# Joining segment sums to place sums by accumulating transfers on GpSimd's queue

## The chip, the cores and the metric

The kernel runs on one core of a Trainium2 chip. The metric is the device time of one execution in microseconds. The core has five engines with queues of their own: PE (TensorE, matmuls into PSUM), DVE (VectorE), ACT (ScalarE), POOL (GpSimd) and SP (SyncE, which here only issues transfers). Each engine works through its queue in order and waits at an instruction until the semaphores it needs have come.

## The reference

128 graphs of 128 nodes with 64 features pass four graph layers. Each layer normalises its input (layer norm, then relu), computes something over the adjacency, and adds it to `x`. The change concerns layer 0:

```
mask = (adj > 0)
h_in = relu(layernorm(x))
h[b,j,k,:] = relu(h_in[b,j] @ W1a + (h_in[b,j] - h_in[b,k]) @ W1b + b1)      # 192 wide
x[b,j] += (sum over k of mask[b,j,k] * h[b,j,k,:]) @ W2 + deg[b,j] * b2
```

With `p = h_in @ (W1a + W1b) + b1` and `q = -h_in @ W1b` the inner term is `relu(p[j] + q[k])`. For every node j one has to sum it over the neighbours k of j, of which there are about 16 of 128 in this data, though some nodes have many more.

Layers 1 to 3 are graph convolutions: layer 1 is three products with the adjacency with relu between, layer 2 one product, a normalisation of rows and one over the whole batch, layer 3 a product with a tanh network.

## The kernel before, in words

The 128 graphs are worked on in 32 groups of four (`G = 4`, `NG = 32`). The main loop, in `network`, runs over the groups; one stream of **tasks** computes the sums of layer 0, and two **side streams** are woven between.

*Tasks.* Instead of all 128 x 128 pairs, the kernel lists the neighbours of each node. A task takes one neighbour of every node: a one-hot matrix (`oh`, `ohn`) picks the q row, PE adds it onto a PSUM tile `blk` that ACT had filled with `psort` (the p rows, sorted so that nodes with more neighbours come first), and the result goes through relu into a running sum `acc`. There are 20 tasks per group, in the order of the list `ORDER`:

- twelve *near* tasks (4 matmuls each), which take a node's first neighbours from each third of the nodes;
- five *full* tasks (12 matmuls each, since q is kept as three bf16 parts), which take one more neighbour of every place;
- three *segment* tasks (12 matmuls each). The 128 rows are split into segments of 76, 33, 11, 4, 2 and 2 (`SEGS`), and each segment holds the first places again, for their further neighbours. So nodes with many neighbours are given more rows. Their p rows `psort_r` are copies of the first rows of `psort`, made by transfers.

The near and full tasks add into `acc0`, in places; the segment tasks add into `acc1`, in segment rows. In `differences` the first task of `acc0` (L582) and all later ones (L586) run on DVE; the first segment task (`FIRST_R`, n = 13) is a relu on ACT (L584). The segment tasks are n = 13, 16 and 18 of 0 to 19.

PSUM has eight banks: three `blk` tiles of two banks each, in turn for the tasks, and a pool `ps` of two banks, from which every side step takes its matmul's output (`ps_rank`, `ps_q`, `ps_sA` and so on). `fill` (L563) refills a `blk` on ACT two tasks ahead; `make_onehot` (L544, L549) builds the one-hot matrices on DVE three ahead.

*The first side stream*, `prepare(g + 1)`: transposes the next group's adjacency, ranks neighbours (`mT`, `ps_rank`, `leftT`, `degs`), sorts nodes by degree (`ps_key`, `ps_place`) and builds `fro`, the matrix that takes places back to nodes, and `to`, its transpose, as `to_b` in bf16 on POOL. It computes q (`ps_q`, written to DRAM and read back as `near_q`), the numbers `num`, and p (`ps_p`). On POOL it computes `db` and adds it to `x`. `fro_r` has rows of `fro` copied once per segment by six transfers on SP's queue (L455).

*The second*, `after_layer0(g - 1)`: `layer0_end` takes the sums from rows to nodes by matmuls with `fro` (for `acc0`) and `fro_r` (for `acc1`), both onto `ps_sA` and `ps_sB`, multiplies by W2 (`ps_o`) and adds to `x`. Then come `layer1` (`ps_ah`, `ps_ag`, `ps_pr`; its last sum onto `x` is on POOL, L644) and `layer2_norm`.

A loop that counts the estimated PE time (`PACE`) and how late each stream is (`N_PREPARE`, `N_AFTER`, `LASTS`, `LAG`) decides after each half task which side step is written next. The order that each engine then gets is set by the scheduler of the language layer when the kernel is built: it may move an instruction ahead of another of its engine, and it sets the waits. Tiles come from pools with a fixed number of buffers: `edge` has two of each (`acc0`, `fro`), `once` has one (`acc1`, `sA`, `sB`).

After the last group comes an end phase: layer 2's normalisation over the batch and layer 3.

Of the kernel before, what the change touches and what calls it, by code (L numbers as in the profile page):

```python
# [9 lines left out]
F32 = mybir.dt.float32  # L10
# [3 lines left out]
AF = mybir.ActivationFunctionType  # L14
ALU = mybir.AluOpType
# [3 lines left out]
P = 128  # L19
F = 64  # L20
G = 4
NP = G // 2
H0 = 192
# [8 lines left out]

THIRD = 42
NEAR = 4
FULL = 5
BLOCKS = 3
SEGS = [76, 33, 11, 4, 2, 2]
STARTS = [sum(SEGS[:s]) for s in range(len(SEGS))]  # L40
LIKE = 4

NEARS = [(t, i) for i in range(NEAR) for t in range(3)]
OTHERS = [(None, i) for i in range(FULL + BLOCKS)]
ORDER = [(NEARS, OTHERS)[k] for k in (0, 1, 0, 1, 0)] * 4
ORDER = [kind[sum(k is kind for k in ORDER[:n])] for n, kind in enumerate(ORDER)]
FIRST, FIRST_R = 0, ORDER.index((None, FULL))
N_PREPARE, N_AFTER = 15, 26
PACE, LAG = 0.88, 2.5
LATE = 18  # L50
LASTS = 1.9
PARTS = [2, 4, 6, 6, 6, 8]
# [2 lines left out]
W = NP * H0  # L55
# [18 lines left out]
def network(ctx, tc, io, out, over=None, x1=None):  # L74
# [4 lines left out]
    nc = tc.nc  # L79
# [21 lines left out]
    def matmul(o, w, x, **kw):  # L101
        spend(w, math.prod(x.shape[1:]), x.dtype)
        return nc.tensor.matmul(o, w, x, **kw)  # L103
# [165 lines left out]
    edge = ctx.enter_context(tc.tile_pool(name="edge", bufs=2, reuse_waits="tile"))  # L269
    once = ctx.enter_context(tc.tile_pool(name="once", bufs=1, reuse_waits="tile"))  # L270
# [83 lines left out]
    xs = [keep.tile([P, G, F], F32, tag=f"x{g}", name=f"x{g}") for g in range(NG)]  # L354
# [41 lines left out]
    sorts, psorts, accs, loaded = {}, {}, {}, {}  # L396
# [5 lines left out]
    def prepare(g):  # L402

        xt, parts_q = xs[g], proj[g % 2]
# [45 lines left out]
        next(ln)  # L450
        fro = edge.tile([P, G, P], F32, tag="fro", name="fro")
        nc.vector.tensor_scalar(flat(fro), pl, place_p, None, ALU.is_equal)  # L452
        fro_r = edge.tile([P, G, P], F32, tag="fro_r", name="fro_r")
        for n, start in zip(SEGS, STARTS):
            nc.sync.dma_start(fro_r[start : start + n], fro[0:n])  # L455
        next(ln)
        yield
        pr = bank("ps_to")
        for b in range(G):
            transpose(pr[:, b * P : (b + 1) * P], fro[:, b, :], ident)  # L460
        to = once.tile([P, G, P], F32, tag="to", name="to")
# [28 lines left out]
        num = edge.tile([P, G, P], BF16, tag="num", name="num")  # L490
# [24 lines left out]
        psort = edge.tile([P, NP, W], F32, tag="psort", name="psort")  # L515
# [6 lines left out]
        psort_r = once.tile([P, NP, W], F32, tag="psort_r", name="psort_r")  # L522
# [3 lines left out]
        extra = once.tile([P, NP, W], F32, tag="rest", name="extra")  # L526
        for b in range(G):
            nc.scalar.activation(of(extra, b), of(psort, b), AF.Relu, scale=empty[:, g, b : b + 1])
        sorts[g], psorts[g] = (num, num_r, fro, fro_r), (psort, psort_r, extra)


    tasks = [(g, n) for g in range(NG if x1 is None else 0) for n in range(len(ORDER))]
# [32 lines left out]
    def differences(t):  # L565
        g, n = tasks[t]
        o, oh, third = columns(t), onehots.pop(t), ORDER[n][0]
        for b in range(G):
            for part in range(3) if third is None else (third,):
                q = (proj if third is None else near_q)[g % 2][:, part]  # L570
                matmul(of(o, b), oh[:, b, :], of(q, b), start=False, stop=True, skip_group_check=True)
            if b == 0:
                fill(t + 2)
                make_onehot(t + AHEAD)
            if b == 1:
                yield
        kind = in_segments(n)
        if n in (FIRST, FIRST_R):
            accs[g, kind] = (once if kind else edge).tile([P, NP, W], F32, tag=f"acc{int(kind)}", name=f"acc{int(kind)}")
        acc = accs[g, kind]  # L580
        if n == FIRST:
            nc.vector.scalar_tensor_tensor(acc, o, 0.0, psorts[g][2], ALU.max, ALU.subtract)  # L582
        elif n == FIRST_R:
            nc.scalar.activation(acc, o, AF.Relu)  # L584
        else:
            nc.vector.scalar_tensor_tensor(acc, o, 0.0, acc, ALU.max, ALU.add)  # L586
        yield

    def layer0_end(g):
        xt, (_, _, fro, fro_r) = xs[g], sorts[g]  # L590

        pA, pB = bank("ps_sA"), bank("ps_sB")
        sA = once.tile([P, G, P], F32, tag="sA", name="sA")
        sB = once.tile([P, NP, P], F32, tag="sB", name="sB")
        sums = ((accs[g, False], fro, True), (accs[g, True], fro_r, False))
        for b in range(G):
            for acc, f, start in sums:
                matmul(pA[:, b * P : (b + 1) * P], of(acc, b, slice(0, P)), f[:, b, :], start=start, stop=not start)
            if b % 2:
                yield  # L600
        nc.scalar.copy(flat(sA), pA)
        for b in range(G):
            for acc, f, start in sums:
                matmul(pB[b % 2 * F : (b % 2 + 1) * F, b // 2 * P : (b // 2 + 1) * P], of(acc, b, slice(P, H0)), f[:, b, :], start=start, stop=not start)
# [114 lines left out]
    else:  # L719
# [12 lines left out]
        for g in range(NG):  # L732
# [4 lines left out]
            for t in range(g * per, (g + 1) * per):  # L737
                for _ in differences(t):
# [3 lines left out]
                    while side:  # L742
                        late, s = max(((s[2] * s[3] / (nyields * s[4]) - s[1], s) for s in side), key=lambda k: k[0])
# [308 lines left out]
```

## Time and profile before

| | |
|---|---|
| time, median of three runs | 1431.54 us (1428.42 to 1433.82) |
| profiled execution: time | 1435.94 us |
| profiled execution: span | 1434.1 us |
| mean granted TensorE clock | 0.973 |
| setup and first `prepare`, to the first `acc` | 57.5 us |
| main loop, to the last `acc` | 1270 us |
| end phase | the rest |
| transfers | 111 MB, 77 GB/s, 27% of the 16 DMA engines |

The span is the profile's own, from the first instruction to the last; the execution's time has 1.8 us more around it. A busy share is that of the whole span. In the lines of the profile, `out<-in` are the program's names without buffer numbers; L103 is the helper by which all matmuls are written, so tile names tell them apart. An f32 matmul shows as two instructions, and since matmuls are pipelined, the durations of neighbours overlap: their starts tell the pace. "Idle before" is the time in which the engine waited just before instructions of a group, with what ended the wait. SPq is SP's queue of transfers.

### The profile page before, as it was taken

The page shows a single profiled execution, that of the slowest core. Times are in us where ns is not written, and L with a number is a line of the kernel's source. Part 1 is how long each engine was busy: PE and PEld are TensorE (multiplying, and loading weights), DVE is VectorE, ACT ScalarE, POOL GpSimd, SP SyncE. Part 2 cuts the span into 40 slices and gives each one's busy share as a digit, 9 for nine tenths or more (in the row PEclk, how much of TensorE's full clock was granted, in tenths as well). Part 3 has the DMA queues.
Part 4 walks back from the last instruction along what each step waited for, and adds up shares of the span by engine and source line. Part 5 has one row for each costly group of instructions (what it writes and reads, how often), then busy time and mean ns, then how long its engine had stood idle before and what let it go on. Part 6 is the DMA issues. An engine that isn't in the chain of part 4 may idle for free. (4 is left out here: it accounts for less than half of the span.)

```text
span 1434.1 us, 29471 instructions
## 1 busy us (share of the span) xinstructions
PE 1251.2 (87%) x11124; PEld 983.2 (69%) x11124; DVE 1186.8 (83%) x2692; ACT 997.8 (70%) x1883; POOL 179.5 (13%) x258
## 2 busy tenths in 40 slices
PE   3788999899999899899989989989989999895788
PEld 1466777777777777777777777767777777773566
DVE  7688888888888988888888888888888888875973
ACT  1577777777777777667777777777777777753783
POOL 3000000000000000000000000000000000003930
PEclk9899999999999999999999999999999999997889
DMA  4353222222222222212222222222222222200345
GB/s 106 107 124 93 77 81 81 75 80 82 74 81 81 74 74 71 72 51 80 81 76 79 81 81 74 81 72 72 65 81 56 71 71 74 67 16 8 87 111 131
DMA packets 108788, 110.97 MB, mean 77 GB/s; under 512 B 42895, under 2 KB 88220, under 8 KB 108636
## 3 DMA queue, kind: packets, MB, share of 16 engines
q1 hardware_dynamic: 108636, 109.00, 27.4%
q8 instruction: 89, 1.46, 0.5%
q14 instruction: 63, 0.52, 0.1%
HBM read 52.70 MB, written 35.29 MB: 61 GB/s over the span
## 5 line engine op out<-in xcount | busy, mean ns | idle before, releaser
L586 DVE SCALAR_TENSOR_TENSOR acc<-blk,acc 128x768 f32<-128x768 f32 x576 | 544.6, 951 | 86.4 <-PE blk L103 52.5
L563 ACT COPY blk<-psort 128x768 f32<-128x768 f32 x544 | 436.0, 805 | 144.9 <-DVE acc L586 125.7
L103 PE MATMUL blk<-q,oh 128*128 128x192 bf16 x3072 | 333.6, 247 | 35.2 <-ACT blk L563 34.3
L103 PEld LDWEIGHTS <-oh 128*128 128x128 bf16 x3072 | 263.8, 99 | 102.9 <-issue 89.0
L103 PE MATMUL blk<-near_q,ohn 128*128 128x192 bf16 x1536 | 196.2, 247 | 8.9 <-ACT blk L563 8.0
L103 PEld LDWEIGHTS <-ohn 128*128 128x128 bf16 x1536 | 132.4, 98 | 40.4 <-issue 30.6
L670 POOL TENSOR_TENSOR y<-y,nrm 128x256 f32<-128x256 f32 x32 | 24.4, 762 | 600.2 <-DVE acc L586 329.3
L563 ACT COPY blk<-psort_r 128x768 f32<-128x768 f32 x96 | 77.6, 809 | 3.7 <-DVE acc L586 3.7
L103 PEld LDWEIGHTS <-ones_b 3*128 3x128 bf16 (+2 forms) x312 | 30.8, 99 | 63.8 <-issue 57.0
L544 DVE TENSOR_SCALAR ohn<-near_n 128x1536 bf16<-128x1536 bf16 x128 | 73.2, 583 | 0.0
L103 PE MATMUL ps_pr<-g,dT 128*128 128x128 f32 x512 | 72.2, 284 | 0.7 <-ACT dT L629 0.3
L103 PE MATMUL ps_ag<-adjT,msg 128*128 128x128 f32 x512 | 71.6, 283 | 0.0
L103 PEld LDWEIGHTS ps_pr<-g,dT 128*128 128x128 f32 x512 | 62.2, 191 | 8.6 <-issue 5.2
L637 ACT COPY msg<-ps_pr 128x512 f32<-128x512 f32 x64 | 37.3, 584 | 42.5 <-PE ps_pr L103 28.3
L484 POOL TENSOR_TENSOR db<-degs,b_all 128x256 f32<-128x256 bf16 x32 | 19.7, 615 | 366.9 <-DVE degs L429 366.9
L103 PEld LDWEIGHTS ps_ag<-adjT,msg 128*128 128x128 f32 x512 | 62.1, 191 | 4.8 <-ACT msg L637 4.4
L103 PE MATMUL ps_p<-wp,hs 128*128 128x384 f32 x128 | 62.1, 568 | 0.0
L582 DVE SCALAR_TENSOR_TENSOR acc<-blk,extra 128x768 f32<-128x768 f32 x32 | 30.6, 958 | 35.4 <-PE blk L103 34.8
L629 ACT ACTIVATE dT<-ps_ag 128x512 f32<-128x512 f32 x96 | 56.6, 590 | 4.5 <-PE ps_ag L103 4.5
L103 PE MATMUL ps_hm<-ident,h 128*64 128x128 f32 x248 | 43.6, 308 | 14.0 <-ACT h L843 14.0
L108 PE MATMUL ps_to<-ident,fro 128*128 128x128 f32 x128 | 21.9, 296 | 37.3 <-DVE fro L452 37.3
L605 ACT COPY sB<-ps_sB 128x256 f32<-128x256 f32 x32 | 11.9, 372 | 60.8 <-PE ps_sB L103 60.8
(221 smaller groups left out, 2696.4 us busy)
## 6 DMA issues: line engine op xcount, KB each, us to landing
q_dram<-q SPq DMA_DIRECT2D x32, 567.0 KB
near_q<-q_dram SPq DMA_DIRECT2D x96, 189.0 KB
near_n<-n_dram SPq DMA_DIRECT2D x96, 126.0 KB
a<-in_adj_dram SPq DMA_DIRECT2D x32, 256.0 KB
adjT_dram<-adjT SPq DMA_DIRECT2D x32, 256.0 KB
adjT<-adjT_dram SPq DMA_DIRECT2D x32, 256.0 KB
psort_r<-psort SPq DMA_DIRECT2D x32, 228.0 KB
fro_r<-fro SPq DMA_DIRECT2D x32, 152.0 KB
```

The source lines that it names most:

```text
L103: return nc.tensor.matmul(o, w, x, **kw)
L108: return nc.tensor.transpose(o, x, i)
L484: nc.gpsimd.tensor_tensor(db, over_f(degs[:, :, 0]), over_g(b2_all), ALU.mult)
L544: nc.vector.tensor_scalar(oh.rearrange("p t b n -> p (t b n)"), near_n[g % 2].rearrange("p t b n -> p (t b n)"), float(i + 1), None, ALU.i ...
L563: nc.scalar.copy(columns(t), psorts[g][in_segments(n)])
L582: nc.vector.scalar_tensor_tensor(acc, o, 0.0, psorts[g][2], ALU.max, ALU.subtract)
L586: nc.vector.scalar_tensor_tensor(acc, o, 0.0, acc, ALU.max, ALU.add)
L605: nc.scalar.copy(flat(sB), pB[:, 0 : NP * P])
L629: nc.scalar.activation(flat(dT), pa, AF.Relu)
L637: nc.scalar.copy(flat(msg), pm)
L670: nc.gpsimd.tensor_tensor(y, y, over_f(nrm), ALU.mult)
```

## The change

It changes how the segment sums `acc1` reach the nodes, and where two of the three segment tasks are summed.

- `fro_r` and its six transfers go, and with them the matmuls of `layer0_end` with `fro_r`.
- The second and third segment task no longer add on DVE. ACT writes the relu into a tile `more` (one buffer), and a transfer on GpSimd's queue adds `more` onto `acc1`.
- After the last segment task five transfers (`FOLDS`) add segment onto segment within `acc1`, until the first 76 rows hold the sum. After the last task of the group a sixth adds these rows onto `acc0`.
- `layer0_end` begins with `yield 2`, uses `acc0` and `fro` alone, and takes `ps_sB`'s bank after `ps_sA`'s.
- `OTHERS` is assigned anew between the two assignments of `ORDER`, and the constants of the weaving change.

```diff
+FOLDS = [(2, 1), (5, 4), (4, 3), (3, 1), (1, 0)]
 
 NEARS = [(t, i) for i in range(NEAR) for t in range(3)]
 OTHERS = [(None, i) for i in range(FULL + BLOCKS)]
 ORDER = [(NEARS, OTHERS)[k] for k in (0, 1, 0, 1, 0)] * 4
+OTHERS = [OTHERS[i] for i in (0, 5, 1, 6, 2, 7, 3, 4)]
 ORDER = [kind[sum(k is kind for k in ORDER[:n])] for n, kind in enumerate(ORDER)]
 FIRST, FIRST_R = 0, ORDER.index((None, FULL))
-N_PREPARE, N_AFTER = 15, 26
-PACE, LAG = 0.88, 2.5
+LAST_R = max(n for n, (t, i) in enumerate(ORDER) if t is None and i >= FULL)
+N_PREPARE, N_AFTER = 16, 27
+PACE, LAG = 0.84, 2.5
...
-        fro_r = edge.tile([P, G, P], F32, tag="fro_r", name="fro_r")
-        for n, start in zip(SEGS, STARTS):
-            nc.sync.dma_start(fro_r[start : start + n], fro[0:n])
         next(ln)
-        yield
+        yield 2
...
         elif n == FIRST_R:
             nc.scalar.activation(acc, o, AF.Relu)
+        elif kind:
+            more = once.tile([P, NP, W], F32, tag="more", name="more")
+            nc.scalar.activation(more, o, AF.Relu)
+            nc.gpsimd.dma_start(acc, more, accum_op=ALU.add)
         else:
             nc.vector.scalar_tensor_tensor(acc, o, 0.0, acc, ALU.max, ALU.add)
+        if n == LAST_R:
+            for s, to in FOLDS:
+                nc.gpsimd.dma_start(acc[STARTS[to] : STARTS[to] + SEGS[s]], acc[STARTS[s] : STARTS[s] + SEGS[s]], accum_op=ALU.add)
+        if n == len(ORDER) - 1:
+            nc.gpsimd.dma_start(acc[0 : SEGS[0]], accs[g, True][0 : SEGS[0]], accum_op=ALU.add)
         yield
 
     def layer0_end(g):
-        xt, (_, _, fro, fro_r) = xs[g], sorts[g]
-
-        pA, pB = bank("ps_sA"), bank("ps_sB")
+        xt, acc, fro = xs[g], accs[g, False], sorts[g][2]
+        yield 2
+
+        pA = bank("ps_sA")
...
-        sums = ((accs[g, False], fro, True), (accs[g, True], fro_r, False))
-        for b in range(G):
-            for acc, f, start in sums:
-                matmul(pA[:, b * P : (b + 1) * P], of(acc, b, slice(0, P)), f[:, b, :], start=start, stop=not start)
-            if b % 2:
-                yield
+        for b in range(G):
+            matmul(pA[:, b * P : (b + 1) * P], of(acc, b, slice(0, P)), fro[:, b, :], start=True, stop=True)
         nc.scalar.copy(flat(sA), pA)
-        for b in range(G):
-            for acc, f, start in sums:
-                matmul(pB[...], of(acc, b, slice(P, H0)), f[:, b, :], start=start, stop=not start)
+        yield
+        pB = bank("ps_sB")
+        for b in range(G):
+            matmul(pB[...], of(acc, b, slice(P, H0)), fro[:, b, :], start=True, stop=True)
```

More of the change, by code (lines that the diff above doesn't have):

```diff
@@ L528, in prepare @@
             nc.scalar.activation(of(extra, b), of(psort, b), AF.Relu, scale=empty[:, g, b : b + 1])
-        sorts[g], psorts[g] = (num, num_r, fro, fro_r), (psort, psort_r, extra)
+        sorts[g], psorts[g] = (num, num_r, fro), (psort, psort_r, extra)
     tasks = [(g, n) for g in range(NG if x1 is None else 0) for n in range(len(ORDER))]
@@ L584, in differences @@
             nc.scalar.activation(acc, o, AF.Relu)
+        elif kind:
+            more = once.tile([P, NP, W], F32, tag="more", name="more")
+            nc.scalar.activation(more, o, AF.Relu)
+            nc.gpsimd.dma_start(acc, more, accum_op=ALU.add)
         else:
             nc.vector.scalar_tensor_tensor(acc, o, 0.0, acc, ALU.max, ALU.add)
+        if n == LAST_R:
[3 more added lines that the diff above has]
+            nc.gpsimd.dma_start(acc[0 : SEGS[0]], accs[g, True][0 : SEGS[0]], accum_op=ALU.add)
         yield
     def layer0_end(g):
-        xt, (_, _, fro, fro_r) = xs[g], sorts[g]
-        pA, pB = bank("ps_sA"), bank("ps_sB")
+        xt, acc, fro = xs[g], accs[g, False], sorts[g][2]
+        yield 2
+        pA = bank("ps_sA")
         sA = once.tile([P, G, P], F32, tag="sA", name="sA")
         sB = once.tile([P, NP, P], F32, tag="sB", name="sB")
-        sums = ((accs[g, False], fro, True), (accs[g, True], fro_r, False))
         for b in range(G):
-            for acc, f, start in sums:
-                matmul(pA[:, b * P : (b + 1) * P], of(acc, b, slice(0, P)), f[:, b, :], start=start, stop=not start)
-            if b % 2:
-                yield
+            matmul(pA[:, b * P : (b + 1) * P], of(acc, b, slice(0, P)), fro[:, b, :], start=True, stop=True)
         nc.scalar.copy(flat(sA), pA)
+        yield
+        pB = bank("ps_sB")
         for b in range(G):
-            for acc, f, start in sums:
-                matmul(pB[b % 2 * F : (b % 2 + 1) * F, b // 2 * P : (b // 2 + 1) * P], of(acc, b, slice(P, H0)), f[:, b, :], start=start, stop=not start)
+            matmul(pB[b % 2 * F : (b % 2 + 1) * F, b // 2 * P : (b // 2 + 1) * P], of(acc, b, slice(P, H0)), fro[:, b, :], start=True, stop=True)
         nc.scalar.copy(flat(sB), pB[:, 0 : NP * P])
```

## The prediction

> **What bounds the kernel now.** I read the page's busy shares, then three periods of the main loop as windows, then the waits.
>
> ```profile
> PE 1251.2 (87%) x11124; PEld 983.2 (69%) x11124; DVE 1186.8 (83%) x2692; ACT 997.8 (70%) x1883; POOL 179.5 (13%) x258
> ```
>
> ```profile
> 440.00:478.20 38.20, 34.97 (x316) 27.68 (x317) 33.20 (x73) 28.35 (x54) 3.55 (x5) 1.00 0.27 76
> 478.20:516.30 38.10, 34.57 (x314) 27.71 (x313) 32.59 (x72) 27.97 (x53) 3.29 (x5) 1.00 0.27 77
> 516.30:554.50 38.20, 34.91 (x314) 27.66 (x314) 33.42 (x73) 28.35 (x54) 3.56 (x5) 1.00 0.26 76
> ```
>
> A period is one group of four graphs. The first `acc` of group 0 stands at 57.5 us, that of group 31 at 1240.3: 31 periods of **38.15 us**. The windows (columns: length, PE, PEld, DVE, ACT, POOL, clock, DMA share, GB/s) show PE busy 34.8 us, DVE 33.1, ACT 28.2. PE sets the period and loses 3.4 us per group in short waits, on the whole-kernel list of waits for example:
>
> ```profile
> ACT blk L563 <- DVE acc L586: 129.4, 145, 2.4
> ...
> PE blk L103 <- ACT blk L563: 45.0, 64, 2.2
> ...
> PE ps_to L108 <- DVE fro L452: 37.3, 32, 1.8
> ```
>
> These are small because the two side streams (`prepare` of the next group, `after_layer0` of the last one) lie evenly between the 20 tasks: whenever one engine waits for a side step, PE has a task to do.
>
> **What the Trainium skill says.** (1) "DMA: Bandwidth & Descriptors", section "Anatomy of one DMA — SWDGE (gpsimd) path": a transfer issued by GpSimd costs some 2.0 us fixed plus its bytes at 436 GB/s. No GpSimd transfer is in this trace. (2) The same page, "Latency and other measured facts": the first byte comes after about 1 us on GpSimd's path, 0.6 us on SP's. SP's hop is in the trace, below. (3) The same page, "Rules for kernel authors": an accumulating transfer reads its destination and writes it later, so one that touches the same bytes has to wait for the earlier one's semaphore. The built order of the changed kernel has these waits. (4) "SBUF — State Buffer", "Who interferes with whom": a VectorE instruction in a two-port mode locks GpSimd out while it writes descriptors. No line of this trace shows such a wait.
>
> **The change, part by part.** *Matmuls with `fro_r` go.*
>
> ```profile
> L103 PE MATMUL ps_sA<-fro_r,acc 128*128 128x128 f32 x256 | 49.5, 275 | 0.0
> ...
> L103 PE MATMUL ps_sB<-fro_r,acc 128*64 128x128 f32 x256 | 26.7, 273 | 0.0
> ```
>
> They overlap, so I take the distances of their starts in the timeline, not the 275 ns: ps_sA pairs start at 700.32, 700.57, 700.79, 701.01 (0.23 each; four pairs per group have `fro_r`), ps_sB fours at 707.41, 707.68, 707.90, 708.12 (0.237; two). That is 0.92 + 0.47 = 1.4 us of PE per group, 45 us in all: PE 34.8 becomes 33.4.
>
> *Two sums move from DVE to ACT.*
>
> ```profile
> L586 DVE SCALAR_TENSOR_TENSOR acc<-blk,acc 128x768 f32<-128x768 f32 x576 | 544.6, 951 | 86.4 <-PE blk L103 52.5 <-ACT sq L299 10.3 <-ACT blk L563 9.9
> ...
> L584 ACT ACTIVATE acc<-blk 128x768 f32<-128x768 f32 x32 | 25.9, 809 | 2.0 <-PE blk L103 1.8
> ```
>
> DVE loses 2 x 0.95 (33.1 to 31.2), ACT gains 2 x 0.81 (28.2 to 29.8). Neither was the bound; worth nothing by itself. *Six `fro_r` transfers* leave SP's queue (4.28 us of issue per group at 711.81); nothing that PE waits for stood behind them, so nothing. *`N_PREPARE`, `N_AFTER`, `PACE`* only shift the order. *The reordering of `OTHERS`* does nothing: `ORDER` already holds the old lists. The segment tasks stay n = 13, 16, 18, so `LAST_R` is 18, next to last.
>
> *Eight accumulating transfers per group* come onto GpSimd's queue: two of `more` (n = 16, 18; 384 KB each), five folds (33, 6, 6, 12, 99 KB), the join (228 KB). In the built order the second `more` transfer waits for the relu of n = 18; fold 2-1 waits for it, 5-4 follows without a wait, 4-3 waits for 5-4, 3-1 for 4-3 and 2-1, 1-0 for 3-1, the join for 1-0, and PE waits for the join before `ps_sA`. **Six transfers in a row**, begun at the end of a group.
>
> What is behind them: `ps` has two banks, given in turn, and `ps_sA` takes one early in the next group. So the built order has no side matmul from about task 4 to task 12 or 13 of the next group; then `ps_sA` comes (in the order before: at task 0 or 1), and with it all the rest: second ranking, placing, `ps_q`, `ps_p`, layers 1 and 2, pressed between six or seven tasks. ACT waits for the join too, at the relu of n = 13, since `acc1` has one buffer. On POOL, `db` and both `x` sums stand behind folds or the join: `db`'s sum is needed only at `ps_o`, and the `x` that the layer norm needs comes after `ps_sA`, so PE's wait covers them. `to_b` stands behind the first `more` transfer in two groups of three; its issue, under 1 us, I count among the stalls.
>
> So the period becomes max(D, W) + R. **R**, from the first `ps_sA` to the end of task 18: PE's steps in the built order sum to 18.7 us (start distances as above; twelve one-hot matmuls take 1.15); with the stalls of before, 38.15/34.8, 20.5. **W**, from there to the next `ps_sA`: 14.7 us of PE, but DVE has 13 `acc`, 7 one-hot builds and the first ranking there, 18.1 us by mean durations, less 0.08 of overlap at 25 starts: 16.1. That tasks without much beside them run at DVE's pace is seen in the last group, where `acc` starts come 1.2 to 1.5 us apart:
>
> ```profile
> 1251.12 0.95 DVE L586 SCALAR_TENSOR_TENSOR acc<-blk,acc 128x768 f32<-128x768 f32 x1
> ...
> 1252.65 0.95 DVE L586 SCALAR_TENSOR_TENSOR acc<-blk,acc 128x768 f32<-128x768 f32 x1
> ...
> 1254.23 0.95 DVE L586 SCALAR_TENSOR_TENSOR acc<-blk,acc 128x768 f32<-128x768 f32 x1
> ```
>
> **D** is the chain from PE's end of task 18 to the join. The trace has one dependent hop on SP's queue, a 126 KB transfer and the next that waits for it:
>
> ```profile
> 720.65 0.35 SPq L492 DMA_DIRECT2D n_dram<-num  x1
> 722.54 0.33 SPq L494 DMA_DIRECT2D near_n<-n_dram  x1
> ```
>
> 1.9 us; 567 KB of `q_dram` at 723.11 to `near_q` at 727.03 takes 3.9. With the skill's 0.4 us more for GpSimd a hop is 2.3; its fixed 2.0 is the low end, 3.2 (descriptors written in turn, destination read too) the high one. I take 2.6 for a small fold. D = handoff and relu 1.5 + `more` 3.9 (2.6, 0.9 for its bytes at the skill's rate, 0.4 for reading the destination) + issue of 2-1 ahead of 5-4 0.9 + three folds 7.8 + fold 1-0 2.8 + join 3.4 = **20.3 us** (16.2 at a hop of 2.0, 24.4 at 3.2). All but the two handoffs are estimates.
>
> Period 20.3 + 20.5 = 40.8, 2.65 more than now, over 31 periods +82 us. After the last group the chain is exposed anew: `ps_sA` was at 1271.7, about 3 us after its last segment sum, and now has to wait some 17 us longer, half of it beside `after_layer0` of group 30: +8. Sum **+90**. The profiled execution took 1435.9 (span 1434.1 and 1.8 around it), 4.4 over the median of 1431.5; on the median, 1522.
>
> **Rivals.** *The chain fits* (faster). If a hop takes 2.0 us or less, D is at most W, and the period is 16.1 + 20.5 = 36.6: -48 us, +4 at the end, 1388. For it: PE and DVE really lose work. Against it: SP's hop of 1.9 us is on a path that the skill calls faster, and six are strung together. The balance is at D = 17.4, a hop of about 2.15 us; if R's stalls are 2 us more, lower. Within 0.5% lies only a narrow strip around it. *GpSimd is slow at this* (far slower): descriptor writing held off by the one-hot builds (0.28 and 0.58 us each, 12 per group), accumulation at half rate: hops of 4 us, D = 29, period 49.7, +366, about 1797. Nothing in the profile speaks for it but that POOL has never issued a transfer here. *The reordering works*: segments at n = 3, 8, 13 would start the chain five tasks (9.5 us) sooner, D would be hidden and the time that of the first rival; the list as built excludes it.
>
> **How the numbers follow.** Chain longer than its cover at hops of 2.2 to 3.2: 0.68, own range 1440 to 1650. Chain fits: 0.18. Balance: 0.06. Very slow hops: 0.08. Faster by over 0.5% (about what a measurement of this kernel can tell from no change) 0.18, within it 0.06, slower 0.76. The range from 1395 to 1650 leaves out the slow rival and the edges.
>
> **What would show it.** Right: the list of waits gets a line of PE at `ps_sA` released by a DMA, some 4 us each; `acc` starts bunch at 1.1 to 1.3 us in the first half of a group; POOL's folds start 2.3 to 3 us apart; PE's busy time falls by about 45 us in a longer span. Wrong: folds under 2.1 us apart and `ps_sA` without a wait, or PE losing its time not there but on ACT's `more` relus or on `to_b`.

## The result, and the profile after

The changed kernel takes **1832.01 us** (median of four runs, 1827.34 to 1838.36) where the kernel before takes 1430.43 beside it: a ratio of **1.281** (95% interval 1.275 to 1.286). The forecast was 1522 with a range up to 1650: the side was right, the time far outside. The profiled execution has a span of 1825.6 us, 391.5 longer than that of before.

Where the 391.5 us lie can be read from the starts of each group's first `acc`. In the kernel after they run from 55.28 us (group 0) to 1600.89 (group 31): 31 periods of **49.86 us** where there were 38.15, so 363 us. From group 31's first `acc` to its `ps_sA` it is 58.8 us where it was 31.4: 27. The end phase is 3.4 us longer, the setup 2.2 shorter.

From the page of the kernel after, the busy shares, GpSimd's own transfer queue (packets, MB, share of the 16 engines) and the chain that ended last:

```profile
PE 1349.6 (74%) x10612; PEld 1001.4 (55%) x10612; DVE 1160.9 (64%) x2628; ACT 1071.3 (59%) x1947; POOL 395.0 (22%) x514
...
q0 software_dynamic: 18432, 37.78, 13.1%
...
PE 28%; DMA 27%; issue 21%; ACT 9%; DVE 8%; POOL 5%; SPq 1%; POOLq 0%; DVEq 0%; ACTq 0%
```

PE has 512 fewer matmuls than before and yet 98 us *more* busy time, and a share of 74% instead of 87%. No engine is near its limit. A quarter of the chain is transfers. A change that lowers the share of PE, VectorE and ScalarE and makes the kernel 28% slower has added waits. The rest of the loss is that PE's own work takes longer: over groups 4 to 27 PE is busy 38.0 us per group and idle 12.5, where it was busy 35.2 and idle 3.5 before, and the mean granted clock there is 0.94 where it was 0.99.

GpSimd's queue in one group (timeline of POOL: start, length, instruction, and in brackets the idle time before and what ended it). The relu of n = 18 starts at 837.53, `ps_sA` at 861.37:

```profile
838.65 0.87 POOL L589 DMA_DIRECT2D acc<-more  x1 [2.26 <-ACT rstd L317]
843.99 1.65 POOL L594 DMA_DIRECT2D acc<-acc  x2 [4.47 <-DMA acc<-more]
845.41 0.88 POOL L485 TENSOR_TENSOR db<-degs,b_all 128x256 f32<-128x256 bf16 x1
846.37 0.93 POOL L486 TENSOR_TENSOR x<-x,db 128x256 f32<-128x256 f32 x1
847.32 0.82 POOL L594 DMA_DIRECT2D acc<-acc  x1
850.02 0.79 POOL L594 DMA_DIRECT2D acc<-acc  x1 [1.88 <-DMA acc<-acc]
852.68 0.82 POOL L594 DMA_DIRECT2D acc<-acc  x1 [1.87 <-DMA acc<-acc]
857.19 0.83 POOL L596 DMA_DIRECT2D acc<-acc  x1 [3.69 <-issue]
```

This is the predicted chain D, one issue after another. Most wait for the landing of the one before; fold 4-3 here also stands behind POOL's own `db` and `x` sums, as in 10 of 29 groups.

Split the period in two: D from the start of the relu of n = 18 to `ps_sA`, and R from there to the next relu of n = 18. Over groups 4 to 27, D is 23.7 us on average and R **27.0**. Three such stretches as windows (columns: length, then busy time of PE, PEld (its weight loads), DVE, ACT and POOL, clock, DMA share, GB/s):

```profile
757.29:790.22 32.93, 26.64 (x184) 19.42 (x185) 16.43 (x46) 16.70 (x36) 2.83 (x4) 0.86 0.30 76
...
812.97:837.53 24.56, 21.01 (x162) 14.19 (x160) 16.62 (x46) 17.30 (x37) 2.83 (x4) 1.00 0.35 86
837.53:861.37 23.84, 15.14 (x137) 12.13 (x137) 16.48 (x25) 14.14 (x21) 7.36 (x9) 0.98 0.35 73
```

The third is a D: PE has 15.1 us of work in 23.8. The second is an R at full clock: 21.0 of PE work in 24.6. The first is an R of 32.9 us; about one in three is as long. In it PE ran at a mean clock of 0.86. The waits of the whole execution:

```profile
PE blk L107 <- ACT blk L564: 231.3, 301, 7.1
...
POOL acc L594 <- DMA acc<-more: 155.6, 32, 8.4
...
POOL acc L594 <- DMA acc<-acc: 126.7, 70, 2.9
...
PE ps_sA L107 <- DMA acc<-acc: 71.2, 23, 6.3
...
ACT more L588 <- DMA acc<-more: 63.6, 12, 6.4
```

The lines (us in total, times, longest) have two ends of the new waiting. PE at `ps_sA` for the join, 71 us, was forecast. The last line wasn't: ScalarE's second relu waits for its buffer `more` until the first transfer has landed, and ScalarE's fills are queued behind it. PE's wait for `blk` fills goes from 45.0 us to 231.3, but only in part for this: 161.2 are left in e9_more2 below, where the relu has two buffers.

The relu waits in 12 groups only, and these go with slow landings. Of the 64 `more` transfers, 33 ran without a `psort_r` copy being issued on SP's queue before they landed; they took 3.9 to 5.2 us (median 4.0). The other 31 took 4.4 to 9.3 (median 7.2). The ten R over 30 us are those of the ten groups whose first `more` transfer has these copies beside it and takes 8.1 to 9.3 us. No run moves the copies alone, so that they are the cause of the slow landings is not shown.

### The profile page after: what moved, and what is told of

Same layout as the page of the kernel before. It is cut to its first block, busy times and chain, and to the rows that moved or that the text cites. A ratio compares the mean times of both kernels' runs of the same rounds, so it can differ in the third digit from the quotient of the medians.

```text
span 1825.6 us, 28815 instructions
## 1 busy us (share of the span) xinstructions
PE 1349.6 (74%) x10612; PEld 1001.4 (55%) x10612; DVE 1160.9 (64%) x2628; ACT 1071.3 (59%) x1947; POOL 395.0 (22%) x514
## 4 chain that ended last, share of the span: by engine, by line
PE 28%; DMA 27%; issue 21%; ACT 9%; DVE 8%; POOL 5%; SPq 1%; POOLq 0%; DVEq 0%; ACTq 0%
DMA acc<-acc 16%; DMA acc<-more 11%; PE blk L107 8%; PE ps_pr L107 5%; PE ps_p L107 3%; PE ps_hm L107 2%; ACT blk L564 2%; PE ps_o L107 2%; PE ps_sA L107 2%; PE ps_ag L107 2%; ACT more L588 1%; PE ps_q L107 1%; DVE acc L591 1%; POOL x L652 1%; POOL acc L594 1%
## 5 line engine op out<-in xcount | busy, mean ns | idle before, releaser
L591 DVE SCALAR_TENSOR_TENSOR acc<-blk,acc 128x768 f32<-128x768 f32 x512 | 487.5, 952 | 73.1 <-PE blk L107 44.0
L107 PE MATMUL blk<-q,oh 128*128 128x192 bf16 x3072 | 345.1, 257 | 160.5 <-ACT blk L564 160.1
L107 PEld LDWEIGHTS <-oh 128*128 128x128 bf16 x3072 | 278.1, 102 | 209.3 <-issue 200.9
L594 POOL DMA_DIRECT2D acc<-acc x160 | 133.0, 894 | 291.8 <-DMA acc<-more 155.6
L589 POOL DMA_DIRECT2D acc<-more x64 | 56.8, 887 | 333.4 <-ACT more L588 271.6
L588 ACT ACTIVATE more<-blk 128x768 f32<-128x768 f32 x64 | 51.7, 808 | 105.5 <-DMA acc<-more 63.6
L107 PE MATMUL ps_sA<-fro,acc 128*128 128x128 f32 x256 | 47.8, 346 | 71.3 <-DMA acc<-acc 71.2
L418 DVE TENSOR_SCALAR mT<-adjT 128x512 bf16<-128x512 f32 x32 | 13.6, 426 | 127.8 <-ACT adjT L396 127.8
L652 POOL TENSOR_TENSOR x<-x,t 128x256 f32<-128x256 f32 x32 | 23.3, 728 | 302.8 <-DVE t L651 302.8
L107 PEld LDWEIGHTS ps_sA<-fro,acc 128*128 128x128 f32 x256 | 41.5, 246 | 76.3 <-issue 72.7
L564 ACT COPY blk<-psort_r 128x768 f32<-128x768 f32 x96 | 77.7, 810 | 9.5 <-DVE acc L591 9.2
```

Of the source, the lines that this page charges most:

```text
L418: nc.vector.tensor_scalar(mT, adjT, 0.0, None, ALU.is_gt)
L564: nc.scalar.copy(columns(t), psorts[g][in_segments(n)])
L588: nc.scalar.activation(more, o, AF.Relu)
L589: nc.gpsimd.dma_start(acc, more, accum_op=ALU.add)
L594: nc.gpsimd.dma_start(acc[STARTS[to] : STARTS[to] + SEGS[s]], acc[STARTS[s] : STARTS[s] + SEGS[s]], accum_op=ALU.add)
L652: nc.gpsimd.tensor_tensor(xt, xt, t, ALU.add)
```

## The experiments

The theory on record was one loop: period = max(D, W) + R. The rival that the experiments brought up is two costs that nearly add: side work held behind `ps_sA`, and `more` on ScalarE by itself. All times are medians; the kernel before was at 1427.9 to 1431.3 beside them. Periods are taken as above.

| kernel | us | ratio to before (95%) | period | clock |
|---|---|---|---|---|
| before | 1430.4 | 1 | 38.15 | 0.973 |
| after | 1832.0 | 1.281 (1.275 to 1.286) | 49.86 | 0.915 |
| e3_hop | 1954.9 | 1.369 (1.359 to 1.379) | 54.08 | 0.868 |
| e1_order | 1726.4 | 1.209 (1.205 to 1.212) | 46.67 | 0.881 |
| e5_moreonly | 1651.4 | 1.156 (1.146 to 1.167) | 44.55 | 0.927 |
| e7_late14 | 1660.5 | 1.163 (1.151 to 1.175) | 44.50 | 0.892 |
| e4_dve | 1650.2 | 1.154 (1.149 to 1.160) | 44.39 | 0.929 |
| e12_dve_late | 1464.5 | 1.025 (1.019 to 1.031) | 38.15 | 0.966 |
| e9_more2 | 1832.0 | 1.282 (1.271 to 1.292) | 49.75 | 0.912 |
| e6_warm | 1872.0 | 1.310 (1.304 to 1.316) | 51.42 | 0.906 |
| e6b_warm | 1929.2 | 1.348 (1.344 to 1.353) | 52.92 | 0.925 |
| e13_nojoin | 1397.3 | 0.978 (0.970 to 0.985) | 37.06 | 0.967 |
| e14_moreorder | **1406.9** | 0.984 (0.980 to 0.989) | 37.24 | 0.976 |
| e15_border | 1421.8 | 0.994 (0.992 to 0.997) | 37.80 | 0.972 |
| e10_best | 1525.6 | 1.068 (1.063 to 1.073) | 40.82 | 0.932 |
| e16_acc2 | 1485.0 | 1.038 (1.034 to 1.042) | 39.33 | 0.952 |
| e16b_acc2late | 1549.6 | 1.086 (1.081 to 1.090) | 41.26 | 0.924 |
| e17_all | 1524.8 | 1.065 (1.062 to 1.068) | 40.53 | 0.933 |

### Is the chain on the path? (e3_hop)

One more serial accumulation of zeros between fold 1-0 and the join (`zero2` is a tile of zeros):

```diff
+            nc.gpsimd.dma_start(acc[0:2, 0, 0:F], zero2, accum_op=ALU.add)   # after the last fold
```

> The kernel after with one more accumulating transfer in the chain, between fold 1-0 and the join: zeros onto two rows of acc1 (256 bytes each), so the sums stay the same. Theory A: the chain is on the path one for one, +2.7 to 3.3 us in 32 groups: +85 to +105, about 1925. If it is not on the path (the period set by the bunched side work alone): under +30.

Measured +123 us against after, 4.2 us in the period, more than either forecast. Over groups 4 to 27 D rises by 2.3 us, about a hop, and R by 2.0. So the chain's length counts, as predicted; that the way back grew as well was the first sign that more than the chain was wrong. The count isn't a clean price of a hop: the built order moved too, with `ps_sA` after 13 or 15 tasks of the next group where it had been 13 or 14, and PE's own wait at `ps_sA` grew by only 0.5 us per group (2.3 to 2.8).

### One part at a time (e1_order, e5_moreonly, e7_late14)

e1_order puts the reordering of `OTHERS` ahead of the line that uses it, so that the segment tiles really stand at n = 3, 8, 13:

```diff
-ORDER = [(NEARS, OTHERS)[k] for k in (0, 1, 0, 1, 0)] * 4
 OTHERS = [OTHERS[i] for i in (0, 5, 1, 6, 2, 7, 3, 4)]
+ORDER = [(NEARS, OTHERS)[k] for k in (0, 1, 0, 1, 0)] * 4
```

> OTHERS is permuted ahead of the first ORDER line, so the segment tasks really stand at n = 3, 8, 13; the same eight transfers. Theory A (the chain of transfers at the end of a group, with the two ps banks holding the side work behind it, is the cost): the chain starts five tasks sooner, about 10 of its 24 us lie beside the end of the group, and most of the 400 us go: 1450 to 1550. Theory B (accumulating transfers disturb the engines or DMA wherever they stand): as many transfers, so still above 1750. Theory C (what costs is ACT: two more relus and their wait for the one buffer of `more`): the relus are now five tasks apart, which frees the wait of 64 us and no more: about 1770.

Measured 1726. It fell between the forecasts: starting the chain five tasks sooner gives back only a quarter of the loss. In the built order `ps_sA` then stands after 3 to 6 tasks instead of 13 or 14, and PE's wait for the join there grew from 71 us to 170. So the run doesn't say how large the rest is; the next ones do.

e5_moreonly is the kernel *before* with `more` for n = 16 and 18, no folds and no join. To make room the one-hots have four buffers instead of five and `lower` shares the place of `mT`; e14_moreorder below has the same two edits and is fast, so they are hardly the cost.

```diff
+        elif kind:
+            more = once.tile([P, NP, W], F32, tag="more", name="more")
+            nc.scalar.activation(more, o, AF.Relu)
+            nc.gpsimd.dma_start(acc, more, accum_op=ALU.add)
```

> The kernel before, with only the two `more` sums on ACT and GpSimd's queue; no folds, no join, fro_r and its matmuls stay (to make room one tile shares its place with another that is dead by then, and the one-hot pool has 4 buffers instead of 5). Theory A: no chain, one transfer of 6 to 9 us ahead of ps_sA: 1430 to 1500. Theory C (the `more` sums are the cost): 1600 or more.

Measured 1651: `more` by itself costs 220 us, with no fold in the kernel. This was the surprise, and it went against the theory on record. e7_late14 is the kernel after with `layer0_end` begun twelve steps later, so that `ps_sA` comes after task 14 and the other side work has the two `ps` banks meanwhile:

```diff
-        yield 2          # first line of layer0_end
+        yield 14
-N_PREPARE, N_AFTER = 16, 27
+N_PREPARE, N_AFTER = 16, 39      # and `fro` in a pool of three buffers
```

> The kernel after, but layer0_end yields 14 instead of 2 ahead of taking its bank (N_AFTER 39 instead of 27; fro gets a third buffer, which this needs), so that ranking, placing and ps_q of the next group are not held behind ps_sA, which now stands at task 14. The chain itself is unchanged. Theory A: the chain of 24 us is covered by side work: 1430 to 1500. A rival to A's second half (only the chain's length counts, not what is held behind it): ps_sA has the same wait, 1750 or more.

Measured 1660, between the two forecasts: 170 us less than after but still 230 over before.

### The two costs crossed (e4_dve, e12_dve_late)

e4_dve takes `more` out of the kernel after (VectorE sums n = 16 and 18 as before) and leaves folds and join; e12_dve_late does both edits, e4's and e7's.

```diff
-        elif kind:
-            more = once.tile([P, NP, W], F32, tag="more", name="more")
-            nc.scalar.activation(more, o, AF.Relu)
-            nc.gpsimd.dma_start(acc, more, accum_op=ALU.add)
```

> The kernel after without `more`: the tiles n=16 and n=18 are summed by VectorE as in the kernel before, the five folds and the join stay. Theory: the chain loses the relu (1.1 us), the issue (0.9) and the 4.5 to 9 us until the next fold leaves, so falls from 23.7 to about 16.5 us; the way back loses the buffer wait and is 23 to 24.5 us; period 39.5 to 41 us, 1475 to 1520. Rival (the folds and the join carry the cost, `more` only its landing of 4 us): 1690 to 1720.

> VectorE sums n=16 and n=18 (no `more`), the five folds and the join stay, and layer0_end begins twelve steps later (ps_sA after task 14 of the next group, `fro` in three buffers), so that the two `ps` banks are free for the other side work while the transfers are on their way. Theory (what the folds and the join cost is the side work that is held behind ps_sA: bare tasks at VectorE's pace ahead of it, TensorE's work behind it): 1420 to 1490. Rival (six transfers per group cost their time on GpSimd and the DMA engines wherever ps_sA stands): 1600 or more, as with e4_dve.

With e7_late14 this makes a square of periods:

| | `more` on ScalarE | sums on VectorE |
|---|---|---|
| bank for `ps_sA` taken early | 49.86 (after) | 44.39 (e4) |
| bank taken twelve steps later | 44.50 (e7) | 38.15 (e12) |

e4 missed both of its forecasts; e12 met the theory's. `more` costs 6.3 us per group alone and 5.5 beside the other cost, the early bank 6.2 and 5.4: they nearly add. It isn't the place of `ps_sA` itself that differs: in the built order it stands after 13 or 14 tasks of the next group in the kernel after, in e7 and in e12 alike (8 or 11 in e4). What differs is whether the other side work has to wait behind its bank.

With both gone, five folds and a join per group are still issued, the list of waits has no line of PE at `ps_sA` for a transfer, and **the period is that of the kernel before**. That doesn't make the transfers free: e12 also lacks the matmuls with `fro_r`, and e13_nojoin below, which has neither those nor any transfer, runs at 37.06. Between the two lie 1.1 us per group, for the folds, the join or the late `ps_sA`; the runs don't tell these apart. The rest of e12's loss lies after the loop: from group 31's first `acc` to the end its span has 221.4 us, that of before 193.8.

What the early bank costs is seen in e4 without the disturbance of `more`. The window from a group's first fold to `ps_sA`, and the one from there to the next group's first fold:

```profile
710.20:728.50 18.30, 11.73 (x106) 9.20 (x106) 15.95 (x26) 10.99 (x17) 6.45 (x9) 1.00 0.31 66
728.50:753.70 25.20, 23.40 (x196) 17.28 (x197) 20.00 (x50) 18.71 (x39) 1.95 (x3) 1.00 0.29 73
```

Ahead of `ps_sA` PE works 11.7 us of 18.3, and VectorE 16.0: bare tasks at VectorE's pace. Behind it PE works 23.4 of 25.2. In the kernel before PE was busy 34.8 and VectorE 33.1 of 38.15 us; here the same work is sorted into a stretch bound by one engine and then a stretch bound by the other. PE waits for the join at `ps_sA` only 77.7 us in all in e4, 2.5 per group, so most of the 6.2 us is something else. The windows speak for the lost interleaving; a part is PE's clock, which over groups 4 to 27 is 0.95 in e4 and 1.00 in e12. No run takes one without the other.

What `more` costs is seen in e7, where PE hardly waits for the chain at `ps_sA` (9.3 us in all). From its waits:

```profile
ACT more L589 <- DMA acc<-more: 137.1, 32, 5.4
```

4.3 us per group as a mean, and some in every group, at the relu of n = 18: its buffer is free only once the transfer of n = 16 has landed, two tasks before. Here that transfer has `psort_r` copies beside it in 31 of 32 groups, and it lands after 8.3 us (median); the transfer of n = 18, with none, after 4.0. ScalarE does its fills in order behind the relu, so PE runs dry too: over groups 4 to 27 it is idle 8.8 us per group where it is 4.4 in e12, as much more as the relu waits. The other 2 us of the 6.3 are PE's busy time, 36.3 for 34.3, at a mean clock of 0.90 for 1.00.

### Would a second buffer do? (e9_more2)

```diff
-            more = once.tile([P, NP, W], F32, tag="more", name="more")
+            more = edge.tile([P, NP, W], F32, tag="more", name="more")
```

> The kernel after, with two buffers for `more` instead of one. Theory (the loop from ScalarE's second relu through the chain to ps_sA and back is the period, and in one group of three the relu's wait for the single buffer lengthens the way back from about 25 to 32 us): the chain keeps its 23.7 us, the way back falls from a mean of 26.4 to about 24, so about 70 us less than after: 1760 (1730 to 1790). Rival (the relu's wait is covered, and the way back is long for TensorE's halved clock alone): within 20 us of after, 1812 to 1850.

`lower` shares the place of `mT` for room. Measured 1832.0, no change at all. That is the rival's number, but the reason is another, and the timeline of POOL has it. In this group the relus of n = 16 and n = 18 start at 926.87 and 929.50, with no wait between them:

```profile
927.95 0.91 POOL L589 DMA_DIRECT2D acc<-more  x1 [14.43 <-ACT more L588]
...
937.33 0.88 POOL L589 DMA_DIRECT2D acc<-more  x1 [7.62 <-DMA acc<-more]
942.17 1.66 POOL L594 DMA_DIRECT2D acc<-acc  x2 [3.96 <-DMA acc<-more]
```

The second transfer now waits for the first, since both accumulate into the same `acc`; POOL waits so in 11 groups, 77.0 us in all. The wait has moved from ScalarE, where it lengthened R, to GpSimd, where it lengthens D: over groups 4 to 27 R falls from 27.0 to 25.1 and D rises from 23.7 to 25.5. "DMA: Bandwidth & Descriptors" in the Trainium skill, section "Rules for kernel authors", says that such a transfer must wait for the earlier one's semaphore; here that wait is 7.6 us long, and a buffer can't remove it; more distance between the two could, or a faster landing of the first.

### More distance, and the rest without transfers (e14_moreorder, e15_border, e13_nojoin)

e14_moreorder is e5_moreonly with the order in force, so that the two `more` stand five tasks apart (n = 8 and 13) and six tasks follow the last one. e15_border is its control: the kernel before with the order alone.

```diff
 OTHERS = [(None, i) for i in range(FULL + BLOCKS)]
+OTHERS = [OTHERS[i] for i in (0, 5, 1, 6, 2, 7, 3, 4)]
```

> The kernel before with two `more` sums, as in e5_moreonly, but with the segment tiles at n=3, 8 and 13: five tasks lie between the two, and seven between the last and the end of the group. Theory (in e5_moreonly the two transfers are serial, since both write `acc`, and the second one's landing is what ps_sA waits for): nothing waits, 1425 to 1460. Rival (ScalarE's two relus or the transfers' own traffic cost): 1560 or more.

> The kernel before with only the interleaved order in force (segment tiles at n=3, 8, 13). A control for e10_best and e14_moreorder. Theory (the order in itself is neutral, and e10_best's 95 us above before is GpSimd's in-order queue): 1425 to 1450. Rival (the order moves VectorE's and TensorE's work together badly): 1500 or more.

Both came out under their forecasts. The order alone gives 0.994; with `more` it is **0.984**, the fastest kernel here that computes everything, and faster than its control (the intervals don't meet). The same 64 relus and 64 transfers of 384 KB that cost 220 us at n = 16 and 18 gain some 15 us at n = 8 and 13: VectorE has two sums less per group, and ScalarE's relu has no wait for a landing left among its waits. The new place gives distance, and it gives more than that: the first transfer, which landed after 5.9 us in e5 (median, with `psort_r` copies beside it in 31 of 32 groups), has none beside it and lands after 3.9. Which of the two frees the relu was not tried apart.

e13_nojoin is the kernel after without any of its transfers, so that the segments' sums never reach the nodes: `more` taken out as in e4, and

```diff
-            for s, to in FOLDS:
-                nc.gpsimd.dma_start(...)
-            nc.gpsimd.dma_start(acc[0 : SEGS[0]], accs[g, True][0 : SEGS[0]], accum_op=ALU.add)
```

> The kernel after with none of its transfers: VectorE sums n=16 and n=18, and the five folds and the join are left out (the segments' sums do not reach the places). What is left of the change is the single sum in ps_sA and ps_sB, PACE, the yields and no fro_r. Theory (only the transfers and where they put ps_sA cost): 1385 to 1430. Rival (the pacing constants or the moved layer0_end cost by themselves): 1480 or more.

Measured 1397: fewer matmuls, `PACE` and the moved `layer0_end` do no harm by themselves; `ps_sA` stands after 3 or 4 tasks here. This is what the join by transfers would gain if it were free.

### Does PE's half clock count? (e6_warm, e6b_warm)

"TensorE: Matmul & The Clock Gate" in the Trainium skill, section "Part 1: The HAM clock gate (the "warmup" mystery)", says that PE falls to half its clock after an idle window of about 3.4 us. Here the trace agrees: after a wait of 6.34 us the eight `ps_sA` matmuls take twice their time. The timeline of PE in the kernel after:

```profile
757.29 2.05 PE L107 MATMUL ps_sA<-fro,acc 128*128 128x128 f32 x8 [6.34 <-DMA acc<-acc]
```

Such a wait isn't the only way to it. In the kernel before, the stretch from 372.8 to 376.2 us ran at a clock of 0.50, and PE's longest wait from 365 to 377 us was 0.7; so these traces don't confirm a threshold.

To price the half clock, both kernels keep PE at work with matmuls into `ps_sA`'s bank, which the real ones overwrite:

```diff
         pA = bank("ps_sA")
+        for _ in range(24):      # e6_warm
+            nc.tensor.matmul(pA, upto, flat(sorts[g][0]), start=True, stop=True)
+        for _ in range(7):       # e6b_warm, instead: reads the segments' sums
+            nc.tensor.matmul(pA, fro[:, 0, :], flat view of accs[g, True], start=True, stop=True)
```

> The kernel after with 24 bf16 matmuls of 128x128x512 per group into ps_sA's bank ahead of the real ones (results overwritten), so that TensorE runs while the join is on its way. They add about 5.3 us of TensorE work per group at the full clock, 165 us in all. Theory (the wait at ps_sA costs a second time, since TensorE then runs its work at half clock: 312 us of half-clock stretches against 80 before): they fill the wait and the clock holds; 1720 to 1800. Rival (the half-clock stretches lie in idle time and cost nothing): the dummies cost what of them sticks out of the wait, 1835 to 1900.

> The kernel after with seven fp32 matmuls of 128x128x512 into ps_sA's bank that read the segments' sums, so that they can't start before the fold 1-0 has landed and run while the join is on its way (about 0.55 us each, 4 us; overwritten by the real ones). In e6_warm the matmuls stood some 10 us too early for that. Theory (TensorE's half clock behind the wait costs a few us per group): 1720 to 1790. Rival (the half-clock work runs beside VectorE's or in slack and costs little): 1810 to 1860.

e6_warm doesn't test it: nothing held its matmuls back, the scheduler put their start some 14 us ahead, and PE waited at `ps_sA` all the same, 2.4 us per group as a mean and up to 6.3. In e6b_warm they stand where they should (timeline of PE):

```profile
740.90 8.42 PE L605 MATMUL ps_sA<-acc,fro 128*128 128x512 f32 x14 [3.36 <-DMA acc<-acc]
749.15 1.05 PE L107 MATMUL ps_sA<-fro,acc 128*128 128x128 f32 x8
```

They took 8.4 us, not the 4 expected, so they stick out of the join's 4.2; but `ps_sA` then runs at full clock, 1.05 us instead of 2.05. Over groups 4 to 27 D grows by 4.3 us and R falls by 1.0, from 27.0 to 26.0. So the half clock behind this one wait is worth about 1 us per group, some 30 us of the 400; a rough price, since the built order moved too (`ps_sA` after 10 to 12 tasks). Both forecasts missed; the rival was nearer.

The half clock as a whole is not priced by this, for most of it stayed: the mean clock of groups 4 to 27 is 0.935 in the kernel after and 0.941 in e6b. In the kernel after PE is busy in half-clock stretches for 5.0 us per group. If all of that work would have taken half the time and nothing else had held it, 2.5 us per group would be gained: an estimate, from the clock record, of what it costs PE at most. How much of it the period pays stays open.

### All parts where nothing waits? (e10_best, e16_acc2, e16b_acc2late, e17_all)

e10_best has e4's and e1's edits, `yield 8` in `layer0_end` with `N_AFTER` 33, and `fro` in three buffers; e16_acc2 changes one line; e16b_acc2late has that line, `yield 14` and `N_AFTER` 39; e17_all is e16b with `more` at n = 8 and 13 (and, for room, one-hots in three buffers and `lower` in the place of `mT`).

```diff
-            accs[g, kind] = (once if kind else edge).tile(...)
+            accs[g, kind] = edge.tile(...)          # e16_acc2: two buffers for acc1
```

> A version meant to beat both: no `more` (VectorE sums two of three segment tiles), the interleaved order in force (segment tiles at n=3, 8, 13, so that the folds run under the last six tasks), ps_sA some nine tasks into the next group, `fro` in three buffers. Theory (the transfers cost nothing where nothing waits for them in order; 1.4 us of fp32 matmuls per group is gone): 1385 to 1420. Rival (GpSimd's queue itself is the cost: six issues of 0.89 us and their landings ahead of the sums of db, x and y, for which TensorE waits): 1450 to 1530.

> e10_best with one edit: the segments' accumulator has two buffers. Theory (what kept e10_best at 1526 is ScalarE's relu of n=3, which overwrites the single buffer that the previous group's join still reads, 22 us after that group's n=13): 1380 to 1430. Rival (GpSimd's in-order queue, six issues per group): 1490 or more.

> e16_acc2 with ps_sA after task 14 instead of task 9. Theory (nothing waits for a transfer in either): within 15 us of e16_acc2, 1380 to 1430. Rival (the late layer0_end squeezes the three layers behind it into too few tasks, as the 34 us of e12_dve_late suggest): 1440 to 1480.

> All parts of the change kept, each where nothing waits for it: order in force (n=3, 8, 13), `more` on ScalarE for n=8 and n=13, folds and join, two buffers for the segments' accumulator, ps_sA after task 14, `fro` in three buffers; one-hots in three buffers instead of five for the room. Theory: below e14_moreorder's 1407, since 1.4 us of TensorE work per group goes as well: 1365 to 1405. Rival (chain from n=13 of some 25 us, or one-hots in three buffers, hold something again): 1430 to 1500.

None reached its theory's forecast; e10_best alone lies in its rival's range. In e10_best the chain of waits goes through the folds, from the sum of n = 13 to the relu of the *next* group's n = 3:

```profile
772.20 0.88 DVE acc L588
...
789.49 0.51 issue
790.00 4.24 DMA acc<-acc
...
794.50 0.82 ACT acc L586
```

That relu overwrites `acc1`, which the join still reads. Two buffers took 41 us off (1526 to 1485), so the single buffer was part of the loss. It isn't all: e16_acc2 has 39.33 per period, and e16b_acc2late, which differs only in a later `ps_sA`, is slower again at 41.26, although the same later `ps_sA` gave 38.15 under the old order (e12). What these two wait for is not settled. GpSimd's queue has as many issues per group in e12, where the period is 38.15, so that the issues alone aren't it. PE's clock can account for most of the gap to e12: with f the mean clock over groups 4 to 27, (1 - f) times the period, an estimate of what half clock takes, is 1.2 us per group in e16 (f = 0.970), 2.6 in e16b (0.939) and nothing in e12 (1.000). Why the clock falls there no run tests; PE's wait for a transfer at `ps_sA` comes to 1.5 us in all in e16, and e16b has none. So the theory that nothing would be left to pay once every landing has time is shown for `more` (e14); e12's loop still lies 1.1 us per group above e13's, and for the whole change the theory failed.

## Why the prediction was wrong

**Right, with its numbers.** *The reordering is dead*: the segments stayed at 13, 16, 18, and putting it in force changed the kernel (e1). *The six-transfer chain is there and its length counts*: e3. *PE's work ahead of `ps_sA`*: forecast 14.7 us, measured 15.1, with bunched `acc` starts. *`fro_r`'s transfers, `PACE`*: no harm in e13, as costed. *Matmuls with `fro_r`*: forecast 45 us of PE; e13, with nothing added, is 33 us below before, so the gain has about that size. It didn't come as forecast: PE's busy time is only 9 us less there (1242.5 for 1251.2), and in the kernel after it is 98 us more where the list of signs had 45 less.

The side was right in part by luck. PE was to wait some 4 us per group at `ps_sA`; it waits 2.3, and the period grew by 11.7.

**D, mis-sized by 3.4 us.** By the means of groups 2 to 30, with the forecast in brackets: relu to issue 1.1 (1.5 with PE's handoff), `more` 5.8 (3.9), the three fold steps 3.6 + 3.0 + 2.8 (8.7 in all), fold 1-0 3.2 (2.8), join 4.2 (3.4): 23.7 for 20.3. The hop of 2.6 us, estimated from SP's queue and the skill's price, was good: 2.7 is the median of the two that follow a small fold. The large transfers were underpriced, `more` most: from 4.2 to 9.3 us until the next fold.

**W, mis-sized by some 5 us.** Forecast 16.1, from VectorE's busy time. With D at 23.7 and only 2.3 of it spent by PE waiting at `ps_sA`, what ran ahead took about 21.4 (means of groups 4 to 27). The stretch that was to cover the chain was nearly as long as the chain.

**R, the term that failed most.** Forecast 20.5: 18.7 of PE and 1.8 of stalls "of before". Measured 27.0. In an undisturbed group at full clock it is 24.6 (24.5 is the mean of all but the long ones), with 21.0 us of PE and 3.5 of idle time: both parts were too small, PE's work by 2.3 us and its stalls by 1.7, 4.1 of the missing 6.5 with rounding. The stalls ratio of before came from an order in which side work and tasks cover each other, and the prediction had itself said that this order was gone. PE's sum was taken from distances of starts in the trace of that order; why the busy time is longer is not shown. The rest of the 6.5 is the one group in three with R near 32 us, where ScalarE's relu waits 5 to 6 us for `more` and PE runs in part at half clock.

**"Worth nothing by itself."** That was said of moving two sums to ScalarE, on the ground that ScalarE is not the bound. The two relus are 1.6 us of ScalarE's time. But the step counted the instruction and not the *buffer* that it has to wait for: 2 us per group in the kernel after (R falls by 1.9 in e9), 4.3 in e7. As a whole `more` costs 5.5 us per group between after and e4; the part that isn't this wait was in the forecast, in D. The list of signs named the wait ("PE losing its time not there but on ACT's `more` relus"), with no price.

**The tail**, forecast +8, is +27: D takes 24.4 of the 58.8 us from group 31's first `acc` to its `ps_sA`, where `ps_sA` had followed the last segment sum after about 3 us. So the chain is nearly all exposed there, and the forecast had half of it covered. e12, whose loop is as long as that of before, has an end 28 us longer too.

**The sum.** Forecast 31 x 2.65 + 8 = 90. Measured 31 x 11.71 + 27, and 1 for setup and end: 391. (D and R above add to 50.7 over the middle groups; the first and last few are shorter, hence the mean of 49.86.)

**The rivals.** *The chain fits* fell: even where PE never waits for it, in e12, the period is 38.15 and not 36.6. *GpSimd is slow at this* came nearest in time (1797) for a wrong reason: hops are 2.7 us, not 4. *The reordering works* would have given 1388; in force it gives 1726.

## What to carry to other kernels

When a sum moves to another engine and a transfer, price the landing: until when does it hold the buffer, which later accumulation into the same tile must wait for it, and what stands in order behind the engine that waits; a second buffer only moved such a wait here, another place in the order removed it (1651 us at n = 16 and 18, 1407 at n = 8 and 13). When a consumer comes to wait, ask what shares its pool of PSUM banks: here the waiting step cost 2.5 us by its wait and 6.2 in all, with the side work held behind its bank. Don't carry a stalls ratio from one order of work to another: measured on the order before it gave 1.8 us, and 3.5 came.

## What the runs showed of the hardware

- Accumulating transfers from SBUF to SBUF on GpSimd's queue, in the kernel after: 0.89 us of GpSimd per issue; small ones (6 to 12 KB) let the next dependent one start after 2.7 us (median), 228 KB take 4.0 us to land, 384 KB 4.4.
- The 384 KB ones take 3.9 to 5.2 us with no `psort_r` copy issued on SP's queue while they run, and 4.4 to 9.3 with such copies. e5, e7 and e14 show the same split: 3.9 to 5.6 us without, 5.2 to 9.1 with; in e1 and e17 single ones without reach 6.2 and 6.5. That the copies cause it was not tried.
- Work of PE behind a wait of 6.3 us ran at half clock (eight matmuls 2.05 us for 1.05), while behind one of 3.0 us (705.60) the same eight took 1.13; half clock also came with no wait of PE over 0.7 us near it. Keeping PE busy over the one wait gave back 1 us per group.
